# A graph layer on one core: shorter packing sums, and single rows fetched by SyncE

## The chip, the cores and the metric

The kernel runs on one core of a Trainium2 chip. The metric is the device time of one execution in microseconds (us), and of several runs the median. Five engines work side by side, each on its own instructions in order: TensorE (PE, its weight loads PEld), VectorE (DVE), ScalarE (ACT), GpSimd (POOL) and SyncE (SP). SyncE, ScalarE and GpSimd can issue DMA transfers; in the profile the issuing side of these queues is called SPq, ACTq and POOLq.

## What is computed

A graph of 50,000 nodes has 1,650,000 directed edges, sorted by destination: 1,600,000 random ones and one self-edge at each node. A node has 160 features, 64 scalars and 32 three-vectors; an edge has four attributes. Each edge makes a message of its source's features and its attributes, the messages are summed at the destination, and a linear map, a ReLU, two residuals and a layer norm follow. Cut to what matters:

```python
ss, vv = s[src], v[src]                      # rows of x, one for each edge
dot = einsum('eui,ei->eu', vv, e1)
out0 = C0 * (ss * e0 @ W1 + dot * INV3 @ W2)
out1 = C1 * (p3 + p4 + p5)                   # bilinear in vv or ss and the attributes
m_agg = segment_sum(concatenate([out0, out1]), dst, num_segments=n)
h = concatenate([m_agg scalars @ Ws, m_agg vectors . Wv])
x = layernorm(x + (x + relu(h)))
```

Since messages are linear in each attribute and in x, the kernel sums attribute times row of x first, and applies the products of the weights to the sums.

## The kernel before

**Units, groups, pairs.** A unit is 128 edges, a group (G = 6) six units whose destinations span at most W = 32 nodes, a pair (PG = 2) two groups and the step of the main loop, and ten pairs (SG = 20 groups) share one load of indices and attributes. There are 2100 groups, so 1050 pairs.

**A pair in the main loop (lines 595 to 629).** `gather` (line 288) has GpSimd fetch for each unit 128 rows of x by an indirect DMA into the tile xg, of which there are six, each for a pair. `spread` (lines 297 and 300) has VectorE build ha, the edges' attributes placed in columns by attribute and destination. `group_sums` (line 325) has TensorE multiply them into ps, six units to a group, and evicts ps to A: on ScalarE (line 330), or, for a packed group, on VectorE (line 334), which adds the self-edges on the way. Every two pairs, `turn` transposes A (line 436, evicted on ScalarE as at, line 439), `apply_weights` multiplies by the weights' products (line 450, evicted on ScalarE as hp, line 454), and, where a block of 128 nodes is complete, `block` adds the parts (line 480) and the norm follows (lines 173 to 192).

**Packed groups.** The first HEAD = 100 groups and the last 20 take their 768 edges as they come. The 1980 groups between are packed: a group is a stretch of L = 787 edges, of which K = 19 self-edges are taken out so that 768 remain. `pack` (lines 341 to 425) does this for 120 groups at once, a group to a partition, in 17 packs of many small VectorE steps. It is a Python generator; each `yield` is a place where the main loop may leave it, and the loop spreads the steps of a pack over the pairs before it is needed. A pack loads the indices and attributes of its groups, marks and counts the self-edges, makes the sums `mine` of the self-edges' attributes by node and attribute (line 389), moves the other edges together by 1, 2, 4, 8 and 16 places (lines 401 to 418), and stores them to DRAM (sd, ad), from where `load` fetches them later (lines 241 and 242). The line to know is the sum's, which runs over half a row, 393 or 394 edges, for each of 32 nodes and four attributes:

```python
for k in range(NK):
    for w in range(W):
        nc.vector.scalar_tensor_tensor(waste[:n, a:e], m[:, q], float(w + 1), pra[:n, a:e, k], ...)
```

For the self-edges `own` (line 305) fetches a group's 32 rows of x, four times over, into the tile xo: SyncE reads the two offsets of a pair into registers (line 310) and issues two DMAs (line 315), three pairs ahead, into four buffers.

**Queues.** SyncE issues every load (indices, attributes, xo, the packs' loads and stores, xt for the residual); ScalarE issues the weights' loads and the output's stores; GpSimd issues the gathers.

**An unused path.** `HELP` maps an engine to a period in units: of every so many units one is fetched by that engine's queue, row by row, each row at an offset held in a register (`fetch`, lines 505 to 516), into a tile of the pool far (three buffers), and `gather` leaves it out. `batches` spreads the 128 rows of such a unit in portions of ROWS over the pairs ahead. HELP is empty before the change.

**Order.** The instructions of an engine do not stand exactly as the Python loop calls them: a scheduler orders them when the program is built, by data and buffers. Lines are those of the kernel before unless the text says otherwise.

Of the kernel before, what the change touches and what calls it, by code (L numbers as in the profile page):

```python
# [37 lines left out]
U8 = mybir.dt.uint8  # L38
# [24 lines left out]
HELP = {}  # L63
HEAD = 100
RP = 120
ROWS = 32
# [28 lines left out]
def tile_gnn_resnorm(ctx: ExitStack, tc: tile.TileContext, x, src, dst, attr, W1, W2, W3, W4, W5, Ws, Wv, out, n_edges):  # L95
# [92 lines left out]
    def norm3(pool, y, mv, rstd, n, row):  # L188
        nc.vector.reciprocal(rstd[:n], rstd[:n])  # L189
        o = pool.tile([P, D], F32, name="o")  # L190
        nc.vector.tensor_scalar(o[:n], y[:n], mv[:n, 0:1], rstd[:n], op0=ALU.subtract, op1=ALU.mult)  # L191
        nc.scalar.dma_start(out[row, :], o[:n])
# [18 lines left out]
    with tc.tile_pool(name="once", bufs=1) as once, tc.tile_pool(name="raw", bufs=2) as rawp, \  # L211
            tc.tile_pool(name="idx", bufs=2) as idxp, tc.tile_pool(name="rows", bufs=6) as rowp, \
            tc.tile_pool(name="far", bufs=3) as farp, tc.tile_pool(name="own", bufs=4) as ownp, \
# [13 lines left out]

        offsets = {}
        evict = nc.vector.tensor_copy if ET.Activation in HELP else nc.scalar.copy

        def load(s):

            n = (min(NG, (s + 1) * SG) - s * SG) * G
            g0 = s * SG
            ra = rawp.tile([P, P, NK], F32, name="ra")
            if NH <= g0 < NH + NPK:
                sd, ad = stored[(g0 - NH) // RP]
                e = slice((g0 - NH) % RP * G * P, ((g0 - NH) % RP * G + n) * P)
                rf = rawp.tile([P, 2, P], F32, name="rf")
                for i in range(2):  # L240
                    nc.sync.dma_start(rf[:n, i, :], sd[i:i + 1, e].rearrange("o (u p) -> (o u) p", p=P))
                nc.sync.dma_start(ra[:n].rearrange("u p k -> u (p k)"), ad[e].rearrange("(u p) k -> u (p k)", p=P))
                return s, n, None, rf, ra
            e = slice(start(g0), start(g0) + n * P)
            ri = rawp.tile([P, 2, P], I32, name="ri")
            nc.sync.dma_start(ri[:n, 0, :], src1[e].rearrange("(u p) o -> u (p o)", p=P))
            nc.sync.dma_start(ri[:n, 1, :], dst1[e].rearrange("(u p) o -> u (p o)", p=P))
            nc.sync.dma_start(ra[:n].rearrange("u p k -> u (p k)"), attr[e].rearrange("(u p) k -> u (p k)", p=P))
            return s, n, ri, None, ra
# [54 lines left out]

        def own(p):

            s, g, ng = pairs[p]
            if not NH <= g < NH + NPK:
                return
            _, at = nc.values_load_multi_w_load_instructions(  # L310
                baseO[0:1, g:g + ng], engines=[ET.SP], min_val=0, max_val=(N - W) * 4 * D,
                skip_runtime_bounds_check_because="an offset of a row of x")
            xo = ownp.tile([P, PG, D], F32, name="xo")
            for i, v in enumerate(at):
                nc.sync.dma_start(xo[:, i, :].bitcast(U8),
                                  xbytes[ds(v, W * 4 * D)].rearrange("(w f) -> w f", w=W).unsqueeze(0)
                                  .to_broadcast([NK, W, 4 * D]))
            owns[p] = xo
# [19 lines left out]
        owns, stored, taken = {}, {}, {}  # L338
        halves = ((0, L // 2), (L // 2, L))

        def pack(c):
# [9 lines left out]
            nc.sync.dma_start(pri[:n, 0, :], src1[e].rearrange("(r e) o -> r (e o)", e=L))  # L351
            nc.sync.dma_start(pri[:n, 1, :], dst1[e].rearrange("(r e) o -> r (e o)", e=L))
            nc.sync.dma_start(pra[:n].rearrange("r e k -> r (e k)"), attr[e].rearrange("(r e) k -> r (e k)", e=L))
            nc.sync.dma_start(pb[:n], base_d[NH + r0:NH + r0 + n])
            yield
            nc.scalar.copy(prs[:n], pri[:n])
# [3 lines left out]
            cum = packp.tile([P, L], F32, name="cum")  # L360
            far = packp.tile([P, L], I32, name="far")
            less = packp.tile([P, L], I32, name="less")
            carry = packp.tile([P, 1], F32, name="carry")
            pbf = packp.tile([P, 1], F32, name="pbf")
            mine = packp.tile([P, 2, NK * W], F32, name="mine")
            waste = packp.tile([P, L], BF16, name="waste")
            nc.vector.tensor_scalar(pbf[:n], pb[:n], float(N - W), None, op0=ALU.min)
            for h, (a, e) in enumerate(halves):
                q = slice(0, e - a)
                nc.vector.tensor_tensor(m[:, q], prs[:n, 0, a:e], prs[:n, 1, a:e], op=ALU.is_equal)  # L370
                nc.vector.tensor_tensor_scan(cum[:n, a:e], m[:, q], zeros[:n].to_broadcast([n, e - a]),
                                             carry[:n] if h else 0.0, op0=ALU.add, op1=ALU.add)
                nc.vector.tensor_copy(carry[:n], cum[:n, e - 1:e])
                yield

                nc.vector.scalar_tensor_tensor(m[:, q], cum[:n, a:e], float(K), m[:, q], op0=ALU.is_le, op1=ALU.mult)
                nc.vector.tensor_scalar(cum[:n, a:e], cum[:n, a:e], float(K), None, op0=ALU.min)
                nc.vector.scalar_tensor_tensor(far[:n, a:e], m[:, q], 0.0, cum[:n, a:e],
                                               op0=ALU.is_equal, op1=ALU.mult)
                yield  # L380
                nc.vector.tensor_scalar(cum[:n, a:e], prs[:n, 1, a:e], pbf[:n], None, op0=ALU.subtract)
                nc.vector.tensor_reduce(packed[:n, 0, 2 * c + h:2 * c + h + 1], cum[:n, a:e], axis=AX.X, op=ALU.min)
                nc.vector.tensor_reduce(packed[:n, 1, 2 * c + h:2 * c + h + 1], cum[:n, a:e], axis=AX.X, op=ALU.max)

                nc.vector.scalar_tensor_tensor(m[:, q], cum[:n, a:e], 1.0, m[:, q], op0=ALU.add, op1=ALU.mult)
                yield
                for k in range(NK):
                    for w in range(W):
                        nc.vector.scalar_tensor_tensor(waste[:n, a:e], m[:, q], float(w + 1), pra[:n, a:e, k],  # L389
                                                       op0=ALU.is_equal, op1=ALU.mult,  # L390
                                                       accum_out=mine[:n, h, k * W + w:k * W + w + 1])
                        if w % 4 == 3:
                            yield
            nc.vector.tensor_copy(counts[:n, c:c + 1], carry[:n])
# [6 lines left out]
            for b in range(K.bit_length()):  # L401
                d = 1 << b
                for a, e in halves:
# [3 lines left out]
                    if d * 2 <= K:  # L407
                        nc.vector.tensor_scalar(less[:n, a:e + d], far[:n, a:e + d], 0x7fffffff - d, None,
                                                op0=ALU.bitwise_and)
                        nc.vector.copy_predicated(far[:n, a:e], mi[:, q], none[:n].to_broadcast([n, e - a]))  # L410
                        nc.vector.copy_predicated(far[:n, a:e], mi[:, r], less[:n, a + d:e + d])
                        yield
# [5 lines left out]
                    yield  # L418
            sd = dram.tile([2, n * G * P], F32, name=f"sd{c}")
            ad = dram.tile([n * G * P, NK], F32, name=f"ad{c}")  # L420
            for i in range(2):
                nc.sync.dma_start(sd[i:i + 1].rearrange("o (r e) -> (o r) e", e=G * P), prs[:n, i, :G * P])
            nc.sync.dma_start(ad.rearrange("(r e) k -> r e k", e=G * P), pra[:n, :G * P])
# [37 lines left out]
        def nodes(b):  # L461
# [4 lines left out]
            nc.sync.dma_start(xt[:nb], x[row, :])  # L466
# [20 lines left out]
        nbatch = P // ROWS  # L487
        batches, helped = {}, {}
        for h, (eng, period) in enumerate(HELP.items()):
            first = PG * G + h * period // 2  # L490
            while True:
# [13 lines left out]
        def fetch(p):  # L505
            for eng, h, q, s, u, i in batches.get(p, []):
                if i == 0:
                    fetched[q, h] = farp.tile([P, D], F32, name=f"xr{h}")
                xr = fetched[q, h]
                _, at = nc.values_load_multi_w_load_instructions(  # L510
                    offsets[s][u:u + 1, i * ROWS:(i + 1) * ROWS], engines=[eng], min_val=0, max_val=(N - 1) * 4 * D,
                    skip_runtime_bounds_check_because="an offset of a row of x")
                for j, v in enumerate(at):
                    r = i * ROWS + j
# [7 lines left out]
        with nc.allow_non_contiguous_dma(reason="one number of each group"):  # L522
            for g0, g1, size in ((0, NH, G * P), (NH, NH + NPK, L), (NH + NPK, NGP, G * P)):
                if g0 < g1:
                    e = slice(start(g0), start(g0) + (g1 - g0) * size)
                    nc.sync.dma_start(base_d[g0:g1], dst1[e].rearrange("(g e) o -> g (e o)", e=size)[:, 0:1])
        baseI = baseB.bitcast(I32)
        nc.sync.dma_start(baseI, base_d.rearrange("g o -> o g").to_broadcast([P, NGP]))
# [4 lines left out]
        zeros = once.tile([P, 1], F32, name="zeros")  # L533
        nc.vector.memset(zeros, 0.0)
# [3 lines left out]
        packed = once.tile([P, 2, max(2 * npacks, 1)], F32, name="packed")  # L538
# [19 lines left out]
        hps, parts, of_nodes, resid, rstds = {}, {}, {}, {}, {}  # L558
# [15 lines left out]
        def do_store(b):  # L574
            norm3(np_, *resid.pop(b), rstds.pop(b), *rows_of(b))
# [7 lines left out]
        STEPS = 10 + NK * W // 2 + 6 * K.bit_length()  # L583
# [11 lines left out]
        for p, (s, g, ng) in enumerate(pairs):  # L595
# [24 lines left out]
            if (g + ng) % QG == 0 or g + ng == NG:  # L620
                after_pair(p + 1, do_turn, c, sums)
                for b in after[c]:
                    after_pair(p + 4, do_block, b)
                    after_pair(p + 5, do_root, b)
                    after_pair(p + 6, do_store, b)
                after_pair(p + 2, do_weights, c)
# [16 lines left out]
        worst = once.tile([P, 7], F32, name="worst")  # L643
        limits = []
        for what, op, limit, cmp in (
                (extremes[:, 0], ALU.min, 0.0, ALU.is_lt), (extremes[:, 1], ALU.max, W - 1.0, ALU.is_gt),
                (packed[:, 0], ALU.min, 0.0, ALU.is_lt), (packed[:, 1], ALU.max, W - 1.0, ALU.is_gt),
                (counts, ALU.min, float(K), ALU.is_lt),
# [4 lines left out]
        wrong = once.tile([P, 7], F32, name="wrong")  # L653
# [76 lines left out]
    with tc.tile_pool(name="edges2", bufs=2) as ep, tc.tile_pool(name="ops2", bufs=2) as op, \  # L730
# [3 lines left out]
        with tc.For_i(0, blocks, 1) as b:  # L734
# [52 lines left out]
            norm3(np_, y, mv, norm2(np_, mv, NBLK), NBLK, row)  # L787
# [33 lines left out]
```

## Time and profile before

| | us |
|---|---|
| median of 3 runs | 15898.5 |
| the three runs | 15871.3, 15898.5, 15898.7 |
| the profiled execution | 15879.8 |
| its span, first to last instruction | 15878.0 |
| GpSimd busy | 11926.1 (75%) |
| TensorE matmul busy, mean granted clock 0.648 | 11902.0 (75%) |
| VectorE busy | 7960.7 (50%) |
| ScalarE busy | 897.9 (6%) |
| 16 DMA engines | gathers' queue 26.9% busy, SyncE's 7.1%, ScalarE's 0.7% |

Busy time counts an engine's own operations. The instructions that issue DMAs, load registers or wait are not in it, so SyncE has no busy time, although it may be occupied. A line of the groups has busy time and mean duration left of the second bar, and right of it the idle time just before these instructions, with what ended most of it; "issue" is idle time in which the profile shows nothing that the engine waited for. A line of the waits names who waited, for whom, the total in us, how often and the longest wait.

### The profile page before, as it was taken

The page shows a single profiled execution, that of the slowest core. Times are in us where ns is not written, and L with a number is a line of the kernel's source. Part 1 is how long each engine was busy: PE and PEld are TensorE (multiplying, and loading weights), DVE is VectorE, ACT ScalarE, POOL GpSimd, SP SyncE. Part 2 cuts the span into 40 slices and gives each one's busy share as a digit, 9 for nine tenths or more (in the row PEclk, how much of TensorE's full clock was granted, in tenths as well). Part 3 has the DMA queues.
Part 4 walks back from the last instruction along what each step waited for, and adds up shares of the span by engine and source line. Part 5 has one row for each costly group of instructions (what it writes and reads, how often), then busy time and mean ns, then how long its engine had stood idle before and what let it go on. Part 6 is the DMA issues. An engine that isn't in the chain of part 4 may idle for free. (4 is left out here: it accounts for less than half of the span.)

```text
span 15878.0 us, 132047 instructions
## 1 busy us (share of the span) xinstructions
PE 11902.0 (75%) x43059; PEld 8781.1 (55%) x43060; DVE 7960.7 (50%) x17460; ACT 897.9 (6%) x2069; POOL 11926.1 (75%) x12611
## 2 busy tenths in 40 slices
PE   7677777777777777777777777777777777777777
PEld 4455555555555555555555555555555555555555
DVE  4565555545454554545454554545455454545422
ACT  0000000000000000000000000000000000000000
POOL 7677777777777777777777777777777777777776
PEclk7666666666666666666666666666666666666666
DMA  3333333333333333333333333333333333333332
GB/s 83 74 86 94 84 82 96 82 95 84 94 83 92 85 82 96 83 96 83 94 85 87 91 82 96 84 94 84 94 83 82 96 82 96 83 93 84 86 83 70
DMA packets 1040422, 1382.05 MB, mean 87 GB/s; under 512 B 233153, under 2 KB 813393, under 8 KB 1035641
## 3 DMA queue, kind: packets, MB, share of 16 engines
q0 software_dynamic: 604800, 1033.00, 26.9%
q1 hardware_dynamic: 378065, 307.98, 7.1%
q10 hardware_dynamic: 56864, 32.58, 0.7%
q8 instruction: 344, 5.64, 0.1%
q14 instruction: 349, 2.86, 0.1%
HBM read 1303.90 MB, written 68.75 MB: 86 GB/s over the span
## 5 line engine op out<-in xcount | busy, mean ns | idle before, releaser
L288 POOL DMA_INDIRECT xg<-in_x,si x12600 | 11924.5, 946 | 3917.0 <-issue 3527.0
L325 PE MATMUL ps<-xg,ha 128*128 128x160 f32 x25200 | 8037.7, 447 | 3686.5 <-DMA xg<-in_x,si 3640.6
L325 PEld LDWEIGHTS ps<-xg,ha 128*128 128x128 f32 x25200 | 5302.5, 266 | 6227.7 <-DMA xg<-in_x,si 6033.2
L334 DVE SCALAR_TENSOR_TENSOR A<-xo,taken,ps 128x160 f32<-128x160 f32 x1980 | 728.8, 377 | 7231.3 <-PE ps L325 7231.3
L389 DVE SCALAR_TENSOR_TENSOR waste<-marks,pra 120x393 bf16<-120x393 f32 (+3 forms) x4352 | 3652.5, 839 | 2.9
L300 DVE TENSOR_TENSOR ha<-hot,pk 128x1536 f32<-128x1536 f32 x1050 | 1830.2, 1744 | 284.1 <-PE ps L325 284.0
L480 PE MATMUL phb<-hp,hot 128*128 128x160 f32 x4544 | 1181.0, 433 | 56.2 <-ACT at L439 52.8
L480 PEld LDWEIGHTS phb<-hp,hot 128*128 128x128 f32 x4544 | 1066.4, 297 | 173.3 <-ACT at L439 172.2
L436 PE MATMUL pt<-ident,A 128*128 128x128 f32 (+1 forms) x4200 | 1051.7, 406 | 100.1 <-ACT hp L454 67.8
L450 PE MATMUL phc<-BWb,at 32*128 32x160 f32 x4200 | 1078.0, 404 | 0.0
L439 ACT COPY at<-pt 128x512 f32<-128x512 f32 (+1 forms) x1050 | 596.9, 579 | 6815.1 <-PE pt L436 6746.4
L450 PEld LDWEIGHTS phc<-BWb,at 32*128 32x128 f32 x4200 | 835.0, 253 | 196.3 <-issue 196.1
L450 PE MATMUL phc<-BWa,at 128*128 128x160 f32 x4200 | 922.6, 374 | 2.3 <-ACT at L439 2.0
L436 PEld LDWEIGHTS pt<-ident,A 128*128 128x128 f32 (+1 forms) x4200 | 700.7, 178 | 302.7 <-ACT hp L454 143.1
L450 PEld LDWEIGHTS phc<-BWa,at 128*128 128x128 f32 x4200 | 847.0, 255 | 35.3 <-ACT at L439 35.3
L297 DVE TENSOR_TENSOR hot<-bank,rel 128x384 f32<-128x384 f32 x1050 | 569.6, 544 | 0.3
L454 ACT COPY hp<-phc 128x160 f32<-128x160 f32 x525 | 153.3, 292 | 6230.2 <-PE phc L450 6171.5
L470 DVE TENSOR_TENSOR hot<-bank,rr 128x768 f32<-128x768 f32 (+2 forms) x391 | 358.8, 918 | 0.1
L389 DVE DVE_READ_ACCUMULATOR waste<-marks,pra 120x1 f32 (+1 forms) x4352 | 342.9, 79 | 0.0
L416 DVE COPY_PREDICATED pra<-marks,pra 120x1572 f32<-120x1572 int32 (+6 forms) x170 | 323.5, 1903 | 0.0
L176 DVE SCALAR_TENSOR_TENSOR y<-phb,xt 128x160 f32<-128x160 f32 x391 | 120.6, 308 | 195.6 <-PE phb L480 195.3
L414 DVE COPY_PREDICATED prs<-marks,prs 120x393 f32<-120x393 int32 (+6 forms) x340 | 181.3, 582 | 0.1
(98 smaller groups left out, 1610.1 us busy)
## 6 DMA issues: line engine op xcount, KB each, us to landing
xg<-in_x,si POOLq DMA_INDIRECT x12600
xo<-in_x SPq DMA_DIRECT2D x1980, 80.0 KB
xt<-in_x SPq DMA_DIRECT2D x390, 80.0 KB
out<-o ACTq DMA_DIRECT2D x390, 80.0 KB
ra<-ad SPq DMA_DIRECT2D x99, 240.0 KB
pra<-in_attr SPq DMA_DIRECT2D x16, 1475.6 KB
ad<-pra SPq DMA_DIRECT2D x16, 1440.0 KB
rf<-sd SPq DMA_DIRECT2D x198, 60.0 KB
```

What stands on the lines that cost most here:

```text
L288: nc.gpsimd.indirect_dma_start(out=xg[:, j, :], out_offset=None, in_=x, in_offset=bass.IndirectOffsetOnAxis(ap=placed[0][:, u + j:u + j + ...
L297: nc.vector.tensor_tensor(hot[:, :n], slotsP[:, 0:W].unsqueeze(1).to_broadcast([P, n, W]), rel[:, u:u + n].unsqueeze(2).to_broadcast([P, n ...
L300: nc.vector.tensor_tensor(ha[:, :n], hot[:, :n].unsqueeze(2).to_broadcast([P, n, NK, W]), pk[:, :, u:u + n].rearrange("p k u -> p u k").un ...
L325: nc.tensor.matmul(ps[:, j // G, :], ha[:, j].rearrange("p k w -> p (k w)"), xr, start=j % G == 0, stop=j % G == G - 1)
L334: nc.vector.scalar_tensor_tensor(A[:, i], xo[:, i], taken[r // RP][:, r % RP:r % RP + 1], ps[:, i], op0=ALU.mult, op1=ALU.add)
L389: nc.vector.scalar_tensor_tensor(waste[:n, a:e], m[:, q], float(w + 1), pra[:n, a:e, k], op0=ALU.is_equal, op1=ALU.mult, accum_out=mine[:n ...
L416: nc.vector.copy_predicated(pra[:n, a:e], mi[:, r].unsqueeze(2).to_broadcast([n, e - a, NK]), pra[:n, a + d:e + d])
L436: nc.tensor.transpose(pt[:f1 - f0, g, :], A[:, i, f0:f1], ident)
L439: evict(at[:, :, :ng].rearrange("f k g w -> f g k w"), pt[:f1 - f0, :ng].rearrange("f g (k w) -> f g k w", w=W))
L450: nc.tensor.matmul(ph[:ng * W], at[:, k, :ng].rearrange("f g w -> f (g w)"), bw[:, k, :], start=i == 0, stop=i == 2 * NK - 1)
L470: nc.vector.tensor_tensor(hot2[:, :len(cs)], slotsP.unsqueeze(1).to_broadcast([P, len(cs), P]), rr[:, :len(cs)].unsqueeze(2).to_broadcast( ...
L480: nc.tensor.matmul(ph[:nb], hot2[:r, i, :nb], hp[:r], start=i == 0, stop=i == len(cs) - 1)
```

## The change

1. SyncE fetches one unit in 45 row by row, in portions of 32 rows (`HELP`, `ROWS`), and issues nothing else.
2. What SyncE issued before goes to ScalarE's queue (`dq`), with one offset load for five pairs instead of one for each pair, and with five buffers for xo instead of four. ScalarE also turns the source indices into row offsets (ro), an existing step that HELP switches on.
3. HEAD falls from 100 to 60, so 2020 groups are packed.
4. The packing sums run over a part of the row: the self-edge of node w is looked for only around place w times the mean degree, 33, from 168 places before it to 234 behind. Two more columns of `packed` record how far self-edges lie from there, and the check at the end covers them; the nodes' loop is outside the attributes' loop, and a pack has other steps between its yields.
5. In a pack, ScalarE makes a copy of the destinations for the comparison, some small steps are merged, and yields are added before the conversion and before the store.
6. The output's store is issued one pair after the norm's last step.

```diff
-HELP = {}
-HEAD = 100
+HELP = {ET.SP: 45}
+HEAD = 60
 RP = 120
-ROWS = 32
+ROWS = {ET.SP: 32, ET.Activation: 16}
...
-            tc.tile_pool(name="far", bufs=3) as farp, tc.tile_pool(name="own", bufs=4) as ownp, \
+            tc.tile_pool(name="far", bufs=3) as farp, tc.tile_pool(name="own", bufs=5) as ownp, \
...
+        own_eng = ET.Activation if ET.SP in HELP else ET.SP
+        dq = nc.scalar if ET.SP in HELP else nc.sync
...
-                    nc.sync.dma_start(rf[:n, i, :], sd[i:i + 1, e].rearrange("o (u p) -> (o u) p", p=P))
+                    dq.dma_start(rf[:n, i, :], sd[i:i + 1, e].rearrange("o (u p) -> (o u) p", p=P))
...
-            _, at = nc.values_load_multi_w_load_instructions(
-                baseO[0:1, g:g + ng], engines=[ET.SP], min_val=0, max_val=(N - W) * 4 * D,
+            if p % OWN == 0:
+                g1 = min(g + OWN * PG, NH + NPK)
+                _, at = nc.values_load_multi_w_load_instructions(
+                    baseO[0:1, g:g1], engines=[own_eng], min_val=0, max_val=(N - W) * 4 * D,
...
+            for _ in range(3):
+                yield
             nc.scalar.copy(prs[:n], pri[:n])
...
-                nc.vector.tensor_tensor(m[:, q], prs[:n, 0, a:e], prs[:n, 1, a:e], op=ALU.is_equal)
+                nc.scalar.copy(m[:, q], prs[:n, 1, a:e])
+                nc.vector.tensor_tensor(m[:, q], prs[:n, 0, a:e], m[:, q], op=ALU.is_equal)
...
-                for k in range(NK):
-                    for w in range(W):
-                        nc.vector.scalar_tensor_tensor(waste[:n, a:e], m[:, q], float(w + 1), pra[:n, a:e, k],
+                for w in range(W):
+                    w0 = max(a, math.floor(degree * w + early))
+                    w1 = min(e, math.ceil(degree * w + late) + 1)
+                    for k in range(NK if w0 < w1 else 0):
+                        nc.vector.scalar_tensor_tensor(waste[:n, w0:w1], m[:, w0 - a:w1 - a], float(w + 1), pra[:n, w0:w1, k],
                                                        op0=ALU.is_equal, op1=ALU.mult,
                                                        accum_out=mine[:n, h, k * W + w:k * W + w + 1])
...
+            for _ in range(2):
+                yield
             sd = dram.tile([2, n * G * P], F32, name=f"sd{c}")
...
-            nc.sync.dma_start(xt[:nb], x[row, :])
+            dq.dma_start(xt[:nb], x[row, :])
...
+        def do_send(b):
+            nb, row = rows_of(b)
+            dq.dma_start(out[row, :], outs.pop(b)[:nb])
...
                     after_pair(p + 6, do_store, b)
+                    after_pair(p + 7, do_send, b)
```

The path that HELP switches on, which stood in the kernel already:

```python
for j, v in enumerate(at):
    r = i * nr + j
    queues[eng].dma_start(xr[r:r + 1, :].bitcast(U8),
                          xbytes[ds(v, 4 * D)].rearrange("(o f) -> o f", o=1))
```

## The prediction, made before the run

> **What bounds the kernel now.** I began with the page's costliest groups: one line keeps one engine in step from end to end, and the others wait for it.
>
> ```profile
> L288 POOL DMA_INDIRECT xg<-in_x,si x12600 | 11924.5, 946 | 3917.0 <-issue 3527.0
> L325 PE MATMUL ps<-xg,ha 128*128 128x160 f32 x25200 | 8037.7, 447 | 3686.5 <-DMA xg<-in_x,si 3640.6
> L334 DVE SCALAR_TENSOR_TENSOR A<-xo,taken,ps 128x160 f32<-128x160 f32 x1980 | 728.8, 377 | 7231.3 <-PE ps L325 7231.3
> L389 DVE SCALAR_TENSOR_TENSOR waste<-marks,pra 120x393 bf16<-120x393 f32 (+3 forms) x4352 | 3652.5, 839 | 2.9
> ```
>
> A gather takes 946 ns on GpSimd, and its idle time is "issue": nobody holds it up. The waits, who waited for whom, say the same, and one more thing:
>
> ```profile
> PEld ps L325 <- DMA xg<-in_x,si: 6033.2, 7101, 8.5
> POOL xg L288 <- issue: 3527.0, 11578, 0.3
> POOL xg L288 <- DVE si L273: 41.8, 2, 36.4
> ```
>
> TensorE waits for gathers. GpSimd's issue gap is 3527.0/11578 = 0.305 us, so a gather costs 0.946 + 0.305 = 1.251 us. The timeline of the middle shows that pitch, whatever VectorE does beside it:
>
> ```profile
> 8001.17 0.95 POOL L288 DMA_INDIRECT xg<-in_x,si  x1 [0.30 <-issue]
> 8002.42 0.95 POOL L288 DMA_INDIRECT xg<-in_x,si  x1 [0.30 <-DMA xg<-in_x,si]
> 8003.67 0.95 POOL L288 DMA_INDIRECT xg<-in_x,si  x1 [0.30 <-issue]
> ```
>
> Sum: 12600 x 1.251 = 15763. The span of 15878.0 has 115 more: 7.6 before the first gather and 35.2 after the last one began (its group runs from 7.6 to 15842.8), one wait of 36.4 for si, and some 36 in longer gathers and short waits, most at the start. The 36.4 lies at 763 to 800 us: the first packed group's indices were not there, because VectorE ended the first pack's compaction at 780.
>
> Last, SyncE, which the page doesn't count as busy: the instructions of the tiles xo, rf, xt and out, and of line 310, by duration (minimum/median/maximum).
>
> ```profile
> L315 SPq MOVE xo<-in_x x1980: 29/38/38, 46.9 to 15637.6; - x198
> L315 SPq DMA_DIRECT2D xo<-in_x x1980: 547/585/708, 47.0 to 15637.7; - x198
> L310 SPq TENSOR_LOAD <-baseO x990: 640/975/3587, 46.0 to 15623.3; - x198
> L241 SPq DMA_DIRECT2D rf<-sd x198: 316/392/1723, 789.5 to 15172.1; - x198
> L466 SPq DMA_DIRECT2D xt<-in_x x391: 327/417/762, 23.1 to 15852.0; - x196
> L192 ACTq DMA_DIRECT2D out<-o x391: 337/338/371, 167.4 to 15866.7; - x196
> ```
>
> A DMA holds its issuing sequencer for 0.3 to 0.6 us. That is the currency in which the change pays.
>
> **What the Trainium skill says.** "Perfetto Trace Analysis", section "DMA Instruction — HWDGE (DVE, Sync)": the recorded time of such a DMA runs from the end of its wait to the end of descriptor generation and of the sequencer's own increments, and excludes the movement; the generator is locked meanwhile. The durations above are thus the sequencer's, and a one-row DMA, with little to generate, should take less than a 128-row one. No row of this trace has one. "DMA: Bandwidth & Descriptors", "Why a DMA increments its semaphore by 16 and not by 1": a DMA is split over the largest number of engines up to 16 that divides its outer dimension. So xt (128 rows) uses 16, rf (120) 15, a single row one. The same page, "Latency and other measured facts", gives a tensor load a floor of about 600 ns; the trace agrees (640 least, 975 median).
>
> **The change part by part.**
>
> *SyncE's rows.* The built program has 279 units fetched by rows: 35712 one-row DMAs and 1116 loads of 32 offsets. GpSimd keeps 12315 gathers instead of 12600 (6 of the 285 go because HEAD 60 packs 40 more groups, whose self-edges need no slot). Off the path: 285 x 1.251 = 357 us, if the rows come in time. GpSimd needs 44 x 1.251 = 55.0 us for its share of 45 units; in that time SyncE must issue 128 rows and 4 loads, or 0.430 us a row.
> Cost of a row: the timeline has two xo DMAs in 1.30 us, 1.30 - 2 x 0.585 = 0.13 between them, of it a MOVE of 0.038; as the second of a pair is a little shorter I take 0.12 around each DMA. The offsets add 0.975/32 = 0.03, if loading 32 costs what loading 2 did. The DMA itself is unknown. xt against rf at their minima: 11 ns for one engine and 8 rows more. If that goes on down to one engine, 0.316 - 14 x 0.011 = 0.16; if nothing of it goes, 0.316. (The 0.40 of a DMA straight after another isn't used: the second xo, behind its MOVE, isn't longer than the first. The 0.585 of xo belongs to a three-dimensional broadcast over 128 rows.) Row: 0.31 to 0.47, and I take the middle, 0.24 + 0.15 = 0.39: 49.9 us a unit against 55.0, 5 us to spare. The decision falls at a DMA of 0.28.
> Their data: 279 x 80 KB come by another queue instead of GpSimd's; the 16 engines are 35% busy. A single row sits on one engine: 128 small packets in 55 us. Cost nothing; the 35% covers it.
>
> *Transfers moved to ScalarE.* 2020 xo at 0.585 + 0.12 are 1.42 ms; about 860 others (xt 391, rf and ra 303, four loads and three stores for each of 17 packs, the start's few) at some 0.45 are 0.39 ms; 204 offset loads at 0.975 are 0.20; the added casts (ro, marks) under 0.1. On ScalarE's 0.90 ms busy and 391 stores this makes about 20% of the span. No bound, but ScalarE runs in order: behind an xo DMA that waits for VectorE's A (SyncE's queue waited 8763 us for that, up to 18.4 at once) stand the copies of at and hp, for which TensorE waits. They belong to later matmuls than the A awaited, so the wait adds little; issue time in front of three copies per four groups adds up to 3 x 1.6 = 4.8 us per two pairs, 2.4 a pair. A pair takes GpSimd 14.7 us and TensorE 11902/1050 = 11.3, so 3.4 are free, and six row buffers hold some 75 us of lead. I cost it at nothing; without that cover each us a pair costs 1050 us. SyncE and ScalarE take completion semaphores from one set of eight, so each DMA waits for the eighth before it: SyncE will stand behind a pack's loads for some us, 17 times, out of its spare 5 us a unit.
>
> *Packing.* 2856 sums on mean 213 elements replace 4352 on 393: by length 2856 x (0.455 + 0.079) = 1.5 ms for 4352 x 0.918 = 4.0. Steady state gains nothing, since VectorE's A waits 7231 us for TensorE. But the head: in the built order of VectorE the first pack's compaction stood behind the 46th pair's ha, just ahead of its need at pair 50; now behind the 13th, need at pair 30. The 36 us wait goes. Late next is the ordinary gather. *Yields, the later store, five own buffers, the limits' two more columns*: order only, or a few us at the end; zero.
>
> Sum against the profiled execution of 15879.8 (span 15878.0): 12315 x 1.251 = 15406, + 7.6 + 35.2 + 36 = 15485, + 1.8 outside = 15487. The median of the runs is 18.7 above the profiled one: **15505**.
>
> **Rivals.**
> *SyncE becomes the bound* (slower). Place: the last unit of every fourth pair, whose matmul waits for xr; every later gather then waits for a row buffer. Price: 279 x 128 = 35.7 us for each ns of a row above 0.430. With a DMA of 0.316: 0.466 x 128 = 59.6 a unit, 4.7 x 279 = 1310, about **16820**. For it: no DMA on either queue took under 0.31, and SyncE's stalls behind ScalarE eat the same reserve. Against: one descriptor on one engine. It decides from 0.28.
> *ScalarE holds TensorE up*: if issue and landing waits take not 2.4 but 3.8 us of each pair, TensorE passes GpSimd by 0.4 x 1050 = 420, and the saving is spent: **15900**, no change. For: in-order copies. Against: the 75 us of lead.
> *The rows do not relieve GpSimd* (pitch set by the data engines) would give about the same; the constant 1.25 at 35% engine load speaks against it, and I count it with the second.
>
> **How the numbers follow.** Forecast 0.58 (own range 15440, no short waits left, to 15620); SyncE bound 0.32, spread from just above the forecast to 16820 and in part beyond; ScalarE or no relief 0.10. About 0.2% is what a measurement of this kernel can tell from no change. Faster: 0.58 + 0.03 of the rivals' near ends = 0.61; same 0.05; slower 0.34. The range 15440 to 16820 leaves out a row dearer than 0.466 (about 0.1) and little below.
>
> **What would show it.** Right: 12315 gathers still 1.25 us apart, the si wait gone, rows under 0.43 us from start to start, no PE wait on xr. Wrong: the row DMA at 0.28 us or more, GpSimd waiting for PE, TensorE waiting for DMA xr; or, for the second rival, PE waiting for ACT at. A pitch other than 1.25 would upset every number here.

## The result, and the profile after

The changed kernel is slower: 18719.4 us (median of 4 runs, 18713.9 to 18721.7) against 15898.6 for the kernel before on the same chip, a ratio of 1.178 (95% interval 1.176 to 1.180). 15505 had been forecast, with a range of 15440 to 16820. The profiled execution of the changed kernel has a span of 18720.0 us. Line numbers are those of the changed kernel from here on (gather 292, matmul 334, A on VectorE 343, a row's offsets 543, a row's DMA 548, xo 324, xt 498, the output's store 615).

The page's costliest groups, in the form known from before (busy and mean duration, then idle time ahead and what ended it):

```profile
L292 POOL DMA_INDIRECT xg<-in_x,si x12315 | 11645.5, 946 | 6958.6 <-issue 3618.4
L334 PE MATMUL ps<-xr,ha 128*128 128x160 f32 x558 | 244.2, 541 | 11232.8 <-DMA xr<-in_x 11232.8
L334 PE MATMUL ps<-xg,ha 128*128 128x160 f32 x24630 | 4058.3, 327 | 30.4 <-DMA xg<-in_x,si 26.0
L419 DVE SCALAR_TENSOR_TENSOR waste<-marks,pra 120x236 bf16<-120x236 f32 (+45 forms) x2856 | 1498.9, 525 | 92.3
```

The gathers are the 12315 forecast and cost what they did, 946 ns. But TensorE, which waited 3641 us for gathers before, now hardly waits for them (26 us) and waits 11233 us for the 279 units that SyncE fetches. The waits (who waited for whom, total us, times, longest) show the rest of the loop:

```profile
PE ps L334 <- DMA xr<-in_x: 11232.8, 279, 80.3
DVE A L343 <- PE ps L334: 9639.6, 670, 39.5
POOL xg L292 <- issue: 3618.4, 11827, 6.5
POOL xg L292 <- PE pt L468: 2245.7, 133, 59.8
POOL xg L292 <- PE ps L334: 1014.6, 250, 58.0
```

Every fetched unit is waited for, 279 times, 40 us on average. GpSimd's pitch is unchanged (3618.4/11827 = 0.306, plus 0.946), but it now stands over 3.2 ms for TensorE, which holds the row buffers: about the excess of 18719 over 15505.

Is SyncE too slow, then? Its own instructions, by duration (minimum/median/maximum):

```profile
L548 SPq MOVE xr<-in_x x35712: 29/29/38, 11.7 to 18697.5; - x200
L548 SPq DMA_DIRECT2D xr<-in_x x35712: 13/208/1946, 18.9 to 18697.5; - x200
L543 SPq TENSOR_LOAD <-ro x1116: 2030/2173/7383, 9.6 to 18685.4; - x186
```

From row to row there are 0.303 us (median of starts). A unit is 128 x 0.303 + 4 x 2.17 = 47.5 us, less than the 49.9 forecast and than the 55.0 of the budget. Yet from one fetched unit's matmul to the next there are 61.75 us in the median and 66.6 in the mean; SyncE stood idle in waits for 5.25 ms. For what it waited, its queue's own waits say:

```profile
SPq L548 <- DMA xo<-in_x: 3154.6, 1502, 61.0
SPq L548 <- DMA pb<-base_d: 447.7, 15, 39.6
SPq L548 <- DMA sd<-prs: 381.4, 18, 36.9
SPq L548 <- DMA ra<-ad: 236.7, 99, 4.7
SPq L548 <- DMA out<-o: 213.2, 168, 32.7
```

Rows of x have no data in common with xo, with the output's store or a pack's loads. They wait for them through the completion semaphores, counters that tell when a DMA has landed. In the built program the DMAs of SyncE and ScalarE take these in turn from one set of eight, so each may go only when the eighth before it in the program's order, on either queue, has landed. One period of the timeline, from one fetched unit to the next (start, duration, engine):

```profile
9013.89 0.87 PE L334 MATMUL ps<-xr,ha 128*128 128x160 f32 x2 [34.47 <-DMA xr<-in_x]
9014.81 1.25 DVE L343 SCALAR_TENSOR_TENSOR A<-xo,taken,ps 128x160 f32<-128x160 f32 x4 [33.43 <-PE ps L334]
9015.51 0.56 ACTq L324 DMA_DIRECT2D xo<-in_x  x1
...
9027.33 0.67 DVE L343 SCALAR_TENSOR_TENSOR A<-xo,taken,ps 128x160 f32<-128x160 f32 x2 [2.90 <-PE ps L334]
9028.32 1.20 ACTq L324 DMA_DIRECT2D xo<-in_x  x2
...
9033.18 0.34 ACTq L498 DMA_DIRECT2D xt<-in_x  x1
...
9034.68 0.34 ACTq L615 DMA_DIRECT2D out<-o  x1
...
9075.81 0.87 PE L334 MATMUL ps<-xr,ha 128*128 128x160 f32 x2 [36.28 <-DMA xr<-in_x]
```

Read it as a loop. When the unit is there, TensorE runs through the 3.75 pairs that had piled up, some 6.8 us each here. ScalarE's transfers follow VectorE step by step: each xo waits for an A to free its buffer, the store for a block's norm. SyncE's first 32 rows trickle out between them, most often held by an xo that has yet to land. In the trace, the second register load of the unit stands at 9036.74, after the last of these rows; the third and fourth at 9050.03 and 9062.42, the next unit's first at 9074.44. So 96 rows in three portions of 12.5 us follow, 37.7 us, for nearly all of which TensorE has nothing to do. 9036.74 - 9013.89 = 22.9 and the tail of 37.7 and 1.4 us to land are the 61.9. The built program says why: in its order, the last 96 rows of nearly every unit stand right ahead of the matmul that needs them, with the transfers of the pairs just before in front of them, although the Python code asks for them two to four pairs earlier. The lock holds both ways: summed over the trace, 271 waits of ScalarE ahead of an xo ended when a row of SyncE landed, 6.4 ms in all. For each of the 17 packs, VectorE's burst and the pack's loads and stores stretch the loop further: 31 of the 278 distances are over 75 us, 1533 us above the median in all.

### The profile page after: what moved, and what is told of

Its sections match the earlier page's. It is cut to its first block, busy times and chain, and to the rows that moved or that the text cites. A ratio compares the mean times of both kernels' runs of the same rounds, so it can differ in the third digit from the quotient of the medians.

```text
span 18720.0 us, 200543 instructions
## 1 busy us (share of the span) xinstructions
PE 6749.0 (36%) x43039; PEld 6325.2 (34%) x43040; DVE 6484.4 (35%) x14632; ACT 914.2 (5%) x2186; POOL 11647.8 (62%) x12327
## 3 DMA queue, kind: packets, MB, share of 16 engines
q1 hardware_dynamic: 71424, 23.00, 0.7%
## 5 line engine op out<-in xcount | busy, mean ns | idle before, releaser
L292 POOL DMA_INDIRECT xg<-in_x,si x12315 | 11645.5, 946 | 6958.6 <-issue 3618.4
L334 PE MATMUL ps<-xg,ha 128*128 128x160 f32 x24630 | 4058.3, 327 | 30.4 <-DMA xg<-in_x,si 26.0
L334 PEld LDWEIGHTS ps<-xg,ha 128*128 128x128 f32 x24630 | 3882.3, 213 | 141.2 <-issue 51.3
L419 DVE SCALAR_TENSOR_TENSOR waste<-marks,pra 120x236 bf16<-120x236 f32 (+45 forms) x2856 | 1498.9, 525 | 92.3
L468 PE MATMUL pt<-ident,A 128*128 128x128 f32 (+1 forms) x4198 | 706.1, 306 | 608.9 <-DVE A L343 578.7
L482 PE MATMUL phc<-BWb,at 32*128 32x160 f32 x4200 | 710.5, 308 | 0.0
L512 PE MATMUL phb<-hp,hot 128*128 128x160 f32 x4538 | 681.2, 299 | 0.0
L482 PE MATMUL phc<-BWa,at 128*128 128x160 f32 x4200 | 658.5, 300 | 0.0
L512 PEld LDWEIGHTS phb<-hp,hot 128*128 128x128 f32 x4538 | 638.0, 190 | 0.6 <-ACT at L471 0.4
L482 PEld LDWEIGHTS phc<-BWb,at 32*128 32x128 f32 x4200 | 583.4, 185 | 90.5 <-issue 90.5
```

Source lines behind the costliest of these rows:

```text
L292: nc.gpsimd.indirect_dma_start(out=xg[:, j, :], out_offset=None, in_=x, in_offset=bass.IndirectOffsetOnAxis(ap=placed[0][:, u + j:u + j + ...
L334: nc.tensor.matmul(ps[:, j // G, :], ha[:, j].rearrange("p k w -> p (k w)"), xr, start=j % G == 0, stop=j % G == G - 1)
L419: nc.vector.scalar_tensor_tensor(waste[:n, w0:w1], m[:, w0 - a:w1 - a], float(w + 1), pra[:n, w0:w1, k], op0=ALU.is_equal, op1=ALU.mult, a ...
L468: nc.tensor.transpose(pt[:f1 - f0, g, :], A[:, i, f0:f1], ident)
L482: nc.tensor.matmul(ph[:ng * W], at[:, k, :ng].rearrange("f g w -> f (g w)"), bw[:, k, :], start=i == 0, stop=i == 2 * NK - 1)
L512: nc.tensor.matmul(ph[:nb], hot2[:r, i, :nb], hp[:r], start=i == 0, stop=i == len(cs) - 1)
```

## The experiments

The theory so far (A): SyncE's rows fit by themselves, but are held in step with ScalarE's transfers, which follow TensorE and VectorE; that closes a loop of a burst and a tail. The rival (B): a unit costs SyncE over 60 us by itself. Four of the runs were on another, slower chip, told last; for the others the kernel before took 15875 to 15886 us.

**Packing alone, and moved transfers alone.**

```diff
 # packing alone
-HELP = {ET.SP: 45}
+HELP = {}
 # moved transfers and packing, no rows: as above, and
-own_eng = ET.Activation if ET.SP in HELP else ET.SP
-dq = nc.scalar if ET.SP in HELP else nc.sync
+own_eng = ET.Activation
+dq = nc.scalar
```

> The changed kernel with HELP empty: the new packing, HEAD 60 and the later store are in, no rows by SyncE, and the other transfers are back on SyncE's queue. Lockstep theory (SyncE's rows can't run ahead of ScalarE's xo transfers, because both take completion semaphores from one set of eight): the packing itself is harmless, GpSimd issues 12594 gathers at 1.251 us, and the one wait for si of 36 us is gone, so about 15850, 0.3% under the kernel before. Rival: the packing part costs something itself (a pack's sums or its store late); then over 16000.

> As the kernel with the packing alone, but the other transfers on ScalarE's queue; SyncE issues nothing. Lockstep theory: without rows nobody waits behind ScalarE's transfers, ScalarE is 80% free, and six row buffers cover its in-order waits: about 15850, the same as the packing alone. Rival (ScalarE's in-order queue holds TensorE up through at and hp): 16500 or more, with PE waiting for ACT at.

Measured: 15848.8 (ratio 0.9983, 0.9976 to 0.9990), and 15836.9 (0.9976, 0.9966 to 0.9986). Both parts are harmless, as forecast; ScalarE's transfers cost nothing while no row stands behind them. The rows alone make the loss, or the rows together with one of these.

**Rows without packs, and rows without xo.**

```diff
 # without packs and their self-edges
-HEAD = 60
+HEAD = 2200
 # without xo, instead: the first pair's tile is kept
             if not NH <= g < NH + NPK:
                 return
+            if one_xo:
+                owns[p] = one_xo[0]
+                return
```

> The changed kernel with HEAD so large that no group is packed: no packs and no xo transfers, rows by SyncE as before, 12894 units. Lockstep theory: with nothing on ScalarE that waits for A, a fetched unit takes SyncE 128 x 0.303 + 4 x 2.2 = 47.6 us against 55.0, GpSimd is the bound again with about 12608 gathers: 15850 to 16200. Rival (SyncE's queue needs over 60 us for a unit by its own issue and landing): 286 x 62 = 17700 or more.

> The changed kernel that fetches xo once, for the first packed pair, and uses that tile for all pairs (left out: the self-edges' rows of all other groups). Packs, their loads and stores, and all rows stay. Lockstep theory: the 6.7 us a unit beyond GpSimd's 55.0 go, and of the about 94 us lost at each of 17 packs a part or all: 15500 with all gone, 17100 with all of the packs' share left. Rival (SyncE's own issue): 18700, nothing changed, since SyncE issues just the same rows.

Measured: 17518.1 (1.1035, 1.0977 to 1.1093) and 18614.5 (1.1726, 1.1676 to 1.1776). Both lie near what the rival foretold (17700 and 18700), and my first theory, that xo alone is what holds the rows, fell with them. But SyncE still stood in waits (3.7 ms without packs), and what it waited for has only changed its name; without packs:

```profile
SPq L548 <- DMA xt<-in_x: 2576.7, 354, 40.0
SPq L548 <- DMA ra<-in_attr: 425.3, 106, 7.9
```

Without xo the same, with 2910.5 us for xt. The row stays at 0.303 us and the median distance at 61.5 and 61.3 us. Without packs, one distance is over 75 us: gathers alone would give 12609 x 1.251 + 80 = 15855, so the loop costs 1.66 ms there, and what is left of the 3.2 ms, some 1.6, belongs to the packs.

**SyncE alone: no transfer on ScalarE's queue.** To the edit without packs come:

```diff
-dq = nc.scalar if ET.SP in HELP else nc.sync
+dq = nc.sync
-            xt = np_.tile([P, D], F32, name="xt")
-            dq.dma_start(xt[:nb], x[row, :])
+            if not xts:
+                xts.append(once.tile([P, D], F32, name="xt1"))
...
-            dq.dma_start(out[row, :], outs.pop(b)[:nb])
+            outs.pop(b)
```

> As the kernel without packs and without ScalarE transfers that wait (it leaves out the x of all other blocks in the sum before the normalization, and the storing of the results), but the loads of indices and attributes too are on SyncE, so that ScalarE's queue holds no transfer in the steady state: a transfer on ScalarE stands behind ScalarE's copies, which wait for TensorE, which waits for xr. Theory A (rows wait for transfers that stand behind ScalarE's work): a unit costs SyncE 128 x 0.303 + 4 x 2.17 + a few transfers = 48 us, under 55.0; TensorE next to never waits for xr; 12609 gathers (there are more without packs) x 1.251 + 80 = 15855, so 15800 to 16000 where the kernel before takes 15900. Theory B (SyncE's queue needs over 60 us a unit by itself): 17400 to 17600. Theory C, from the second chip (there the kernel before itself takes 19073): rows are issued at 1 us and more each while gathers run: 128 x over 0.7 us makes over 90 us a unit, 26000 and more, if this chip behaves like that one.

Measured: 15891.8 (1.0011, 1.0001 to 1.0020), 1626 us less than without packs. The waits of TensorE, of GpSimd and of SyncE's queue:

```profile
PE ps L334 <- DMA xr<-in_x: 510.7, 25, 32.6
POOL xg L292 <- issue: 3649.4, 11970, 0.3
```

```profile
SPq L551 <- ACT A L339: 610.3, 40, 24.3
SPq L551 <- ACT ro L263: 207.4, 34, 20.3
```

TensorE waits for xr 25 times in place of 283, and GpSimd sets the time again. This decides for A against B. Three kinds of transfer went from ScalarE's queue at once (xt, the stores, the loads), so it doesn't say which of them is enough; nor was a kernel run in which the two queues have completion semaphores of their own. SyncE's waits were 1.10 ms, so a unit with its few other transfers took it (15888.6 - 1096.7)/285 = 51.9 us; 55.0 is enough, but not by much.

**All transfers back on SyncE's queue** (nothing left out; the edit is `dq = nc.sync` and `own_eng = ET.SP` in the changed kernel).

> The changed kernel with one part undone: all other transfers, and the register loads of the self-edges' offsets, are back on SyncE's queue, beside the rows. Nothing is left out. Theory A: a unit costs SyncE 47.5 us for the rows and some 11 transfers at 0.3 to 0.6 us and a register load, 53 to 55 us against 55.0; no transfer stands behind ScalarE's copies any more, but each now holds the rows up while it waits for its own buffer: 15600 to 17500, taken 16500, so faster than the changed kernel's 18719. Theory B (61.4 us a unit are SyncE's own): 67 us a unit and more, 19000 to 20500, slower than 18719.

Measured: 17849.8 (1.1246, 1.1227 to 1.1264). Above the expectation of A, faster than the changed kernel as A had it. SyncE is full here: it waits 0.99 ms in all, and (17849.4 - 988.4)/279 = 60.4 us a unit are its own work. I had put both parts at too little: the rows are about 51 us in place of 47.5 (a row every 0.320 us, a register load 2.43), the eleven transfers with their MOVEs, gaps and register loads some 9 in place of 6 to 7. So at one unit in 45 SyncE can't carry both, but moving the transfers to ScalarE cost more than leaving them: it closed the loop.

**What holds ScalarE's transfers?** Its copies ahead of them (A1), or their own buffers (A2)?

```diff
 # more buffers (xt and the offsets get pools of their own, 4 and 3; the blocks' other tiles 2)
-tc.tile_pool(name="own", bufs=5) as ownp
+tc.tile_pool(name="own", bufs=8) as ownp
 # copies on VectorE
-evict = nc.vector.tensor_copy if ET.Activation in HELP else nc.scalar.copy
+evict = nc.vector.tensor_copy
```

> The changed kernel with more buffers for what ScalarE's transfers fill: eight in place of five for xo, four for xt in a pool of its own (three before), three in place of two for the offsets; the other tiles of the blocks have two in place of three to make room. Theory A1 (ScalarE's copies stand ahead of its transfers and wait for TensorE): no change, 18400 to 18900. Theory A2 (the transfers wait for their own buffers, that is for VectorE's A a few pairs back): xo goes out before the burst ends, so much of the 37 us tail goes: 15800 to 17500.

> The changed kernel with the copies at, hp and A on VectorE in place of ScalarE, so that next to nothing on ScalarE's queue waits for TensorE any more; about 1050 x 0.6 + 525 x 0.3 = 0.8 ms more for VectorE, which is idle two thirds of the time. Theory A1: transfers go as soon as their buffers are free, 15600 to 17500. Theory A2: no change, 18400 to 19000; a copy behind a pack's sums on VectorE may add some.

> Both of the last two together. Theory A1 and A2: about as the better one of the two. Theory A3 (either of the two is enough to hold the transfers): only this one is fast, 15600 to 17000. If all three stay at 18400 and more, the rows' place in the program's order behind the transfers of pairs just before is enough by itself, whatever holds these.

Measured: 18818.9 (1.1847, 1.1798 to 1.1895), 18793.3 (1.1831, 1.1792 to 1.1869), and both together 18845.8 (1.1864, 1.1818 to 1.1910). Nothing is gained. For the copies that is an answer: A1 by itself falls, since without them the loop is the same. The buffers were not put to the test. With eight of them, the built order has each xo right behind the A that frees its buffer, just as with five; it is only fetched eight pairs ahead in place of five. The kernel with both changes shows it, after a fetched unit's matmul at 8983.65 and in SyncE's waits (there xo is line 326, A 345, a row 550):

```profile
8984.56 1.25 DVE L345 SCALAR_TENSOR_TENSOR A<-xo,taken,ps 128x160 f32<-128x160 f32 x4 [35.49 <-PE ps L336]
8985.26 6.84 ACTq L326 DMA_DIRECT2D xo<-in_x  x6
```

```profile
SPq L550 <- DMA xo<-in_x: 3223.1, 1733, 61.8
SPq L550 <- DMA out<-o: 148.5, 109, 9.8
```

So A2 and A3 stay open: the transfers still wait for their buffers, and the rows for the transfers. An output's store also stands in front of the last 96 rows in this order and can't go before its block is done, but the rows waited little for it. A kernel with its xo taken out of the place behind A, and nothing left out, was not run.

**Wider spacing** (one number in HELP).

> One unit in 60, nothing else, again, for a chip on which the kernel before takes 15900. 12391 gathers x 1.251 + 80 = 15580 if the rows are in time. Theory A: five pairs at 6.5 us and 37 us make 70 us against 73.8, no slack for the packs' stalls of up to 94 us: 15600 to 17200, taken 16500. Theory B (61.4 us whatever the spacing): 15580 to 15900.

> One unit in 75, nothing else. 12430 gathers x 1.251 + 80 = 15630 if the rows are in time. A chain of 6.25 pairs at 6.5 us and at most 37 us makes 78 us against 92.6 that GpSimd gives; the 15 us spare a unit take a pack's stall of about 94 us, less the 75 us that six row buffers hold, within a unit or two: 15630 to 15750, below the 15662 of one in 90 if no more than 30 us are lost to the packs.

> One unit in 90, nothing else, again, for a chip on which the kernel before takes 15900. 12460 gathers x 1.251 + 80 = 15665 if the rows are in time. Theory A: 7.5 pairs at 6.5 us and at most 37 us make 86 us against 111: 15650 to 16100, taken 15700, below both kernels. Theory C (rows slow while gathers run): 128 x 0.7 + 9 = 99 us and up against 111: 15665 to 17500.

The distances are those of the fetched units' matmuls; the chain is P/12 pairs x 6.5 + 37; GpSimd gives (P - 1) x 1.251.

| one unit in | chain | GpSimd gives | distance, median (mean) | time | ratio (95%) |
|---|---|---|---|---|---|
| 45 | 61 | 55.0 | 61.8 (66.6) | 18719.4 | 1.178 (1.176 to 1.180) |
| 60 | 70 | 73.8 | 69.7 (76.7) | 16185.0 | 1.0197 (1.018 to 1.0214) |
| 75 | 78 | 92.6 | 88.6 (93.8) | 15839.6 | 0.9972 (0.9962 to 0.9982) |
| 90 | 86 | 111.3 | 112.4 (111.4) | 15661.5 | 0.9866 (0.985 to 0.9882) |

At 60 the median is the chain's, and the packs take the mean above what GpSimd gives: (76.7 - 73.8) x 208 = 600 us, the excess over 15580. At 75 I had expected at most 15750; the packs still cost 1.2 us a unit, 200 us; the trace has 19 stalls of GpSimd of over 1.75 us, 223 us in all, each within 90 us of where a pack's compaction begins. At 90 the time is the 15665 worked out, and less than both kernels: 213 us under the kernel before on that chip. Its waits:

```profile
PE ps L334 <- DMA xr<-in_x: 3839.4, 132, 62.3
POOL xg L292 <- issue: 3621.2, 11883, 0.5
POOL xg L292 <- PE ps L334: 127.5, 395, 2.2
```

TensorE still waits for 132 of 139 fetched units, but GpSimd doesn't feel it: TensorE catches up between them, and six row buffers bridge the rest.

**On a slower chip.** There the kernel before itself took 19073. The kernel without waiting transfers is that with SyncE alone, but with the loads of indices and attributes on ScalarE; one in 240 spreads its rows over the last 90 units.

```diff
-at = [int(first + i * period / nbatch) // (PG * G) for i in range(nbatch)]   # one in 240
+at = [int(first + period - 90 + i * 90 / nbatch) // (PG * G) for i in range(nbatch)]
```

> The rows as in the changed kernel (one unit in 45 on SyncE), no packs at all (all groups read their edges as the others do), and ScalarE's queue without any transfer that has to wait for TensorE or VectorE: x is loaded into xt once and reused, and the output is written once, at the start, from that tile. It leaves out the x of all other blocks in the sum before the normalization, and the storing of the results. Only the loads of the indices and attributes (three in ten pairs) stay on ScalarE's queue. Theory A, the rows wait for ScalarE's transfers: SyncE's rows take completion semaphores in turn with ScalarE's transfers, and those stand in the program's order before the last hundred rows of a unit and wait for TensorE and VectorE to have gone past the unit before; with nothing there that waits, a unit costs 128 x 0.303 + 4 x 2.17 = 47.5 us of SyncE, under the 55.0 that GpSimd gives, and the time falls from 17518 (the kernel without packs) to 15450 to 15800, with 55 us between fetched units and next to no wait of TensorE for xr. Theory B, SyncE's queue needs over 60 us a unit by itself (issue, register loads and landing): 17400 to 17600, 61.5 us between fetched units, as in the kernel without packs.

> One unit in 60 in place of one in 45, nothing else. 12391 gathers x 1.251 + about 80 us around them = 15580 if the rows are in time. A unit gives SyncE 59 x 1.251 = 73.8 us. Theory A: TensorE still stands some 37 us before each fetched unit (the last hundred rows can only start once the transfers of the pairs before have gone), and the chain of five pairs at 6.5 us and 37 us makes 70 us, just under 73.8; the packs' stalls have no slack to go into, 17 x up to 94 us: 15600 to 17200, taken 16500. Theory B: a unit costs SyncE 61.4 us however it is spaced, 12 us spare a unit take the packs' stalls within some units: 15580 to 15900.

> One unit in 90, nothing else. 12460 gathers x 1.251 + about 80 us = 15665 if the rows are in time. In the built order three quarters of a unit's rows now stand some two pairs or more before their use. Theory A: a chain of 7.5 pairs at 6.5 us and at most 37 us makes 86 us against the 111 us that GpSimd gives; the packs' stalls fit into a unit or two: 15650 to 16100, taken 15700. Theory B: 61.4 us a unit against 111: 15665 to 15700. Both expect no loss against the kernel before; it tells whether SyncE's rows save their gathers at all when they are in time, 140 x 1.251 = 175 us less than with packing and moved transfers alone (15837 to 15849).

> One unit in 240, its rows asked for over the last 90 units before it as in the kernel with one in 90. In the built order all its rows stand over twelve pairs before their use. 12548 gathers x 1.251 + about 80 us = 15778. Theory A and B: 15770 to 15800, no wait of TensorE for xr; if TensorE still waits for rows here, both are wrong and a row's landing is what is late.

Measured: 27305 (1.4324, 1.4271 to 1.4377), 26953 (1.4146, 1.4123 to 1.4170), 23330 (1.2243, 1.2223 to 1.2263) and 19100 (1.0019, 1.0007 to 1.0030). Every expectation missed, and for a reason that neither theory has: on this chip TensorE's and SyncE's instructions at times come in steps of some 0.7 us (with one unit in 240, rows started 0.7, 1.4, 2.1 or 2.8 us apart more often than at distances between), while GpSimd's pitch is the 1.251 us of the other chips. TensorE in that kernel:

```profile
9001.86 0.43 PE L482 MATMUL phc<-BWa,at 128*128 128x160 f32 x1 [1.80 <-issue]
9003.96 0.43 PE L334 MATMUL ps<-xg,ha 128*128 128x160 f32 x1 [1.67 <-issue]
```

A matmul every 2.1 us, with nothing that it waits for in the trace; rows there started 1.4 us apart in the median. What does it is open. I draw nothing from these four times on the change; the two that mattered were run again on a chip of the usual speed, as shown, and the one in 240 was not.

## Why the prediction was wrong

*The bound and its pitch*: right. The changed kernel has the 12315 gathers, and the median pitch was 1.251 or 1.252 us in every run; the 15665 for one in 90 rests on it.

*The row's own cost*: near enough, with errors that offset each other. The DMA took 0.208 us against 0.24 and the gap around it 0.095 against 0.12, but the offsets 0.068 a row (2.17 us for 32) against 0.03. That is 47.5 us a unit against 49.9; with SyncE alone, its few transfers included, 51.9. "The decision falls at a DMA of 0.28" set the turning point in the time of issue, which did not decide. What the prediction drew from the Trainium skill's "Perfetto Trace Analysis", section "DMA Instruction — HWDGE (DVE, Sync)", that a one-row DMA holds the sequencer for less than a 128-row one, held: 208 ns in the median, against 327 at least for xt's 128 rows.

*The moved transfers*: here it failed. The waits of SyncE behind ScalarE's transfers were put at next to nothing, in the sentence "each DMA waits for the eighth before it: SyncE will stand behind a pack's loads for some us, 17 times, out of its spare 5 us a unit". The mechanism was seen and its places were not. I counted the packs' loads, which are rare, and not the xo, xt and stores of the pairs between, which come late because they follow VectorE; and I took the rows to be issued where the code asks for them, not where the built order puts them. SyncE stood 5.25 ms in 2769 gaps of over 0.15 us, 19 us a unit. Worse, a wait that ends with the progress of TensorE can't be paid out of spare time: it starts the rows only when TensorE is about to need them. At a pack it was no "some us" either: 1533 us in 31 distances.

*Packing*: right. The sums cost 1.50 ms of VectorE and 0.24 for reading them, 1.7 against the 1.5 forecast; nothing gained in the steady state (the ratio of packing alone is 0.9983), and the wait of 36.4 us for si at the first pack is gone; the one wait for si that is left, 17.0 us, is at the start, where the first gather now begins at 19.9 us in place of 7.6.

*The rivals*: "SyncE becomes the bound" names the right place (the fetched unit's matmul, then the row buffers) with the wrong price. A row of 0.466 us was to give 16820 (its own sum, (59.6 - 55.0) x 279, is 1283 and not 1310, so 16790); the row took 0.303 and the time was 1900 us beyond. "ScalarE holds TensorE up" fell with the moved transfers alone, and "the rows do not relieve GpSimd" with the unchanged pitch.

## What to carry to other kernels

Before a second queue's DMAs are counted as free, look in the built order at what stands in front of them and shares their completion semaphores: a transfer that waits for the consumer turns a prefetch into a loop of burst and tail, however much spare time the issuing engine has. Compare that loop's length with the period, not the issue time with the budget. Where the loop can't be cut, stretch the period until it is shorter than the bound with room for the stalls: one unit in 90 gained 1.3% (0.2% of it also came with packing and moved transfers alone) where one in 45 lost 18%.

## What the runs showed of the hardware

- A one-row DMA held SyncE for 208 ns in the median, against 392 for 120 rows and 417 for 128. It was 228 in the kernel with SyncE alone and 225 with all transfers on SyncE's queue; why is open, but not that gathers never paused there, since at one in 90 they hardly paused either and it was 208. The rows' queue moved 71,424 packets for 35,712 rows, two a row, so a row was not split over the 16 engines.
- A register load took at least 0.64 us for 2 values (kernel before), 1.14 for 10 (packing alone) and 2.03 for 32 (changed kernel); the medians are 0.975, 2.26 and 2.17. So more values cost more at the least, but the median did not grow from 10 to 32. The Trainium skill's "DMA: Bandwidth & Descriptors", section "Latency and other measured facts", gives a floor of about 600 ns for a tensor load, which the least of these agrees with.
- The mean recorded matmul of ps (line 325 before, 334 after) fell from 447 to 327 ns where TensorE worked in bursts rather than at the gathers' pace, at much the same mean granted clock (0.648 and 0.667).
- Two chips gave the kernel before 15.9 and 19.1 ms. The steps of 0.7 us were seen in other kernels on the slower one; whether they make the difference is open.
